# Mixing over 64 nodes as two 64-row products on the two halves of TensorE's rows

## The chip, the cores and the metric

The kernel runs on one core of one Trainium2 chip. The metric is the device time in microseconds of one execution, from the first to the last instruction. Before the change it was 2570.01 us (median of 3 runs, 2565.66 to 2570.18).

## The reference

The input `x` has 128 batches of 64 nodes with 256 features, and `adj` is one weighted 64 x 64 graph. Four graph layers follow one another, each of the form

```python
x = _layernorm(x + layer(x, adj))
```

What matters here is that each layer multiplies by a 64 x 64 matrix over the nodes, the same for every batch. Layer 0 does it three times, between three weight matrices (256 to 512 to 1024 to 256 features):

```python
def _slconv(x, adj, S, W):              # S is adj as well: weighting = adj * adj
    support = jnp.einsum('bnf,fh->bnh', x, W)
    weighting = adj * S
    return jnp.einsum('nm,bmh->bnh', weighting, support)
```

Layer 1 multiplies by the eigenvectors U of the graph's Laplacian (transposed, and back again), around two small dense layers. Layer 2 multiplies by `adj` twice, each time with a 256 x 256 weight and relu, and then runs LSTMs over windows of 1 to 4 nodes. Layer 3 is attention along the graph: scores h h^T within a batch, a softmax and a weighted sum. All arithmetic is in float32.

## The kernel before

**Tiles and groups.** The 8192 rows (128 batches x 64 nodes) are 64 tiles of 128 rows, so a tile holds two batches: batch h = 0 on the upper 64 partitions, h = 1 on the lower 64. Four tiles are a group, and there are 16 groups. `X` keeps all rows in on-chip memory for the whole kernel.

**Mixing.** Multiplying by the 64 x 64 matrix is called mixing. It is done for both batches of a tile at once, by a 128 x 128 matrix that has the 64 x 64 matrix twice on its diagonal and zeros elsewhere: `sqT2` (adj squared elementwise, transposed), `adT2`, `u2` and `ut2`. The transposed mixing, with which this case deals, takes 128 columns of features of a tile as the stationary operand (the weights that TensorE loads) and moves the 128 columns of the mixing matrix through. The result has features on the partitions and (tile, batch, node) along the free dimension, which is what the dense layer behind it needs. `mm` (L718) issues one product and adds its estimated time to `now[0]`, the planner's clock. A float32 product is two records in the profile, each with a weight load (`PEld`) and a matmul (`PE`).

**Where it occurs.** In layer 0, `mixed` (L750) makes one chunk of 128 features at a time: four products, one for each tile, fill a PSUM bank (`ps`, six of them), and ScalarE copies it out (L755). It runs with two chunks on X (into `m1`) and with four on `h1` (into `m2`). In layers 1 and 2, another `mixed` (L941) makes two chunks, eight products in two banks; VectorE copies one bank out (L951) and ScalarE the other (L952). It runs once with `u2` and twice with `adT2` in each group. So a group has 48 mixing products, and the 16 groups have 768.

**Another mixing, which stays.** At the end of layer 0 the mixing isn't transposed: `sqT2` is the stationary operand, and 512 columns are moved (`ps<-s,sqT` in the profile, issued right behind L855). Its results are added to X on VectorE (L861), and a layer norm on ScalarE follows.

**What sets the order.** TensorE's order is written out by a planner in Python (`manual_schedule`, L869 and L1195). Each group is a generator that issues some instructions and then yields the time on the planner's clock from which it may go on. In layer 0 two groups are under way at once, later three (`WAYS`). The planner always takes the first group that is due, and moves the clock on if none is. Delays such as `now[0] + 1.5` or `+ MIXED` leave time for copies, in which other groups fill TensorE. In layer 0, `between` (L708), which `mm` calls, threads in the instructions of an eigenvalue computation (`eigen`) that layer 1 needs. Its products are small, most of them on 128 rows and some on 64. In layer 0 VectorE's order is fixed by hand as well.

**A product of another shape.** The scores of layer 3 (L1140) are on 128 rows, but have 64 columns of weights, and write the upper or lower 64 partitions of a bank. They use the left and the right half of TensorE's columns.

Of the kernel before, what the change touches and what calls it, by code (L numbers as in the profile page):

```python
# [15 lines left out]
N = 64  # L16
# [516 lines left out]
P = 128  # L533
# [33 lines left out]
def scalar_norm(tc, pool, x, half, spare):  # L567


    nc = tc.nc  # L570
    S, G = nc.scalar, nc.gpsimd
    nm, va, rs, nb = (pool.tile([P, 2], F32, name=f"sn_{n}") for n in ("nm", "va", "rs", "nb"))

    def total(out, t, func, **kw):
        S.activation(spare[0](), x[:, t, :], func, accum_out=out[:, t:t + 1], **kw)  # L575

    def root():
        G.tensor_scalar(rs, va, 1.0 / D, EPS, op0=ALU.mult, op1=ALU.add)
        G.tensor_tensor(rs, rs, half[:, :2], ALU.pow)
        G.tensor_tensor(nb, nm, rs, ALU.mult)  # L580

    def apply(t):
        S.activation(x[:, t, :], x[:, t, :], AF.Identity, bias=nb[:, t:t + 1], scale=rs[:, t:t + 1])

    return ([lambda t=t: total(nm, t, AF.Identity, scale=-1.0 / D) for t in range(2)] +
            [lambda t=t: total(va, t, AF.Square, bias=nm[:, t:t + 1]) for t in range(2)] + [root] +
            [lambda t=t: apply(t) for t in range(2)])
# [8 lines left out]
def kernel(  # L596
# [26 lines left out]
    V, S, PE = nc.vector, nc.scalar, nc.tensor  # L623
    NT = ROWS // P
# [4 lines left out]
    def tl(pool, shape, tag, **kw):  # L629
        uid[0] += 1  # L630
        return pool.tile(shape, F32, tag=tag, name=f"{tag}_{uid[0]}", **kw)
# [9 lines left out]
    psa = phase_a.enter_context(tc.tile_pool(name="psa", bufs=1, space=bass.MemoryType.PSUM))  # L641
# [12 lines left out]
    for h in range(2):  # L654
        hs = slice(h * N, (h + 1) * N)
# [24 lines left out]
    sqT2 = keep.tile([P, P], F32, name="sqT2")  # L680
# [23 lines left out]
    now = [0.0]  # L704
# [3 lines left out]
    def between():  # L708
        while eig and eig[0] <= now[0]:
            try:  # L710
                eig[0] = next(eig[1])
            except StopIteration:
                eig.clear()
        if norms and due[0] <= now[0]:
            norms.pop(0)()
            due[0] = now[0] + 1.6

    def mm(out, lhsT, rhs, start=True, stop=True):  # L718
        PE.matmul(out, lhsT, rhs, start=start, stop=stop)  # L719
        now[0] += 2 * max(0.00084 * rhs.free_size(), 0.112)  # L720
        between()

    def run(out, pairs):
        for i, (lhsT, rhs) in enumerate(pairs):
            mm(out, lhsT, rhs, i == 0, i == len(pairs) - 1)

    def relu(dst, src):
        S.activation(dst, src, AF.Relu)  # L728
# [14 lines left out]
    def behind(name, g):  # L743
        while done[name] < g:
            yield now[0] + 0.3

    def layer0(g):
        xs = X[:, 4 * g:4 * g + 4, :]

        def mixed(dst, src, nf, more, then=None):  # L750
            for c in range(nf):
                p = tl(psa, [P, 512], "ps", bufs=6)
                for t in range(4):
                    mm(p[:, t * P:(t + 1) * P], src[:, t, c * P:(c + 1) * P], sqT2)
                S.copy(dst[:, c, :], p)  # L755
                if then and c == nf - 1:
                    done[then] = g
                yield now[0] + (more if c == nf - 1 else 0.0)

        yield from behind("first", g - 1)  # L760
        m1 = tl(pa, [P, 2, 512], "m1")
        yield from mixed(m1, xs, 2, 1.4)
        yield from behind("mixed", g - 1)
        h1 = tl(pa, [P, 4, 512], "h1")
        for t in range(4):
            p = tl(psa, [P, 512], "ps", bufs=6)
            run(p, [(m1[:, k, t * P:(t + 1) * P], aw1[:, k, :]) for k in range(2)])
            relu(h1[:, t, :], p)
            if t == 3:
                done["first"] = g  # L770
            yield now[0] + (2.1 if t == 3 else 0.0)
        if g == 0:
            VL.tensor_sub(T3, B22, B12)
            VL.tensor_sub(T1, B12, B11)
            VL.tensor_sub(T2, B22, T1)
            VL.tensor_sub(T4, T2, B21)
        yield from behind("second", g - 1)
        m2 = tl(pa, [P, 4, 512], "m2")
        yield from mixed(m2, h1, 4, 1.4, "mixed")
        A11, A12, A21, A22 = (m2[:, k:k + 2, r:r + 256] for r in (0, 256) for k in (0, 2))  # L780
        ss = tl(pa, [P, 4, 2, 256], "ss")
        S1, S2, S3, S4 = (ss[:, i] for i in range(4))
        VL.tensor_add(S1, A21, A22)
        VL.tensor_sub(S2, S1, A11)
        VL.tensor_sub(S3, A11, A21)
        VL.tensor_sub(S4, A12, S2)
        yield from behind("third", g - 1)
        h2 = tl(pa, [P, 8, 512], "h2")

        def product(w, a, j):  # L790
            p = tl(psa, [P, 2, 256], "ps", bufs=6)
            for i in range(2):
                cols = slice((2 * j + i) * P, (2 * j + i + 1) * P)
                run(p[:, i, :], [(w[:, k, cols], a[:, k, :]) for k in range(2)])
            return p

        def quarter(j, r, c):
            return h2[:, 4 * c + 2 * j:4 * c + 2 * j + 2, r * 256:(r + 1) * 256]

        def join(j, r, c, x, y, op=ALU.add):  # L800
            VL.tensor_tensor(quarter(j, r, c), x, y, op)
            relu(quarter(j, r, c), quarter(j, r, c))


        late = None
        for j in range(2):
            p1 = tl(pa, [P, 2, 256], "p1", bufs=2)
            u2, u3 = (tl(pa, [P, 2, 256], n) for n in ("u2", "u3"))

            def one(p, p1=p1):  # L810
                S.copy(p1, p)

            def six(p, p1=p1, u2=u2):
                VL.tensor_add(u2, p1, p)

            def seven(p, u2=u2, u3=u3):
                VL.tensor_add(u3, u2, p)

            def five(p, j=j, u2=u2, u3=u3):
                join(j, 1, 1, u3, p)  # L820
                VL.tensor_add(u2, u2, p)

            def four(p, j=j, u3=u3):
                join(j, 1, 0, u3, p, ALU.subtract)

            def three(p, j=j, u2=u2):
                join(j, 0, 1, u2, p)

            def two(p, j=j, p1=p1):
                join(j, 0, 0, p1, p)  # L830

            for then, w, a in ((one, B11, A11), (two, B21, A12), (six, T2, S2), (seven, T3, S3), (four, T4, A22),
                               (five, T1, S1), (three, B22, S4)):
                p = product(w, a, j)
                if norms:
                    norms.pop(0)()
                if late:
                    late[0](late[1])
                late = then, p
                if j == 1 and then is three:  # L840
                    done["second"] = g
                yield now[0]
        late[0](late[1])
        s3 = tl(pa, [P, 4, D], "s3")
        for t in (2, 0):
            p = tl(psa, [P, 2, D], "ps", bufs=6)
            for i in range(2):
                for k in range(0, 8, 4):
                    for c in range(k, k + 4):
                        mm(p[:, i, :], h2[:, c, (t + i) * P:(t + i + 1) * P], aw3[:, c, :], c == 0, c == 7)  # L850
                    if t + i == 1 and k == 4:
                        done["third"] = g
                    yield now[0]
            S.copy(s3[:, t:t + 2, :], p)
        yield now[0] + 1.5  # L855
        for t in (2, 0):
            p = tl(psa, [P, 2, D], "ps", bufs=6)
            mm(p, sqT2, s3[:, t:t + 2, :])
            yield now[0] + 0.4
            x2 = xs[:, t:t + 2, :]  # L860
            VL.tensor_add(x2, p, x2)  # L861
            norms.extend(scalar_norm(tc, small, x2, half, spare))
# [72 lines left out]
    def ps4(shape=(P, 512)):  # L935
        return tl(psb, list(shape), "ps")

    def as3(t, a):
        return t.rearrange("p (a b) -> p a b", a=a)

    def mixed(src, rhs, ready):  # L941

        dst = as3(work(), 2)
        ps = [ps4() for _ in range(2)]
        for t in range(4):
            if t % 2 == 0:
                yield ready[t // 2]
            for c in range(2):
                mm(ps[c][:, t * P:(t + 1) * P], src[:, t, c * P:(c + 1) * P], rhs)
        with tc.high_priority(offset=1500):  # L950
            V.tensor_copy(dst[:, 0, :], ps[0])  # L951
        S.copy(dst[:, 1, :], ps[1])  # L952
        yield now[0] + MIXED
        return dst

# [296 lines left out]
```

## Time and profile before

| | |
|---|---|
| median of 3 runs | 2570.01 us |
| span of the profiled execution | 2566.4 us |
| layer 0, from the start to about | 875 us |
| layers 1 to 3, from there to the end | 1691 us |
| granted TensorE clock, mean | 0.994 |
| mixing from X in layer 0, `sqT,X` | 256 records |
| mixing from h in layer 0, `sqT,h` | 512 records |
| mixing in layers 1 and 2, `u,X`, `adT,X` and `adT,w` | 256 records each |
| one such matmul, median | 275 ns |
| one such weight load, median | 192 ns |
| ScalarE copy of a bank in layer 0, L755 | 575 ns, 96 of them |
| VectorE and ScalarE copy of a bank later, L951 and L952 | 689 and 586 ns, 48 each |

How to read it: a line of a group or a timeline has the time, the engine, the line of the kernel, the operation, the tiles by name (`ps<-sqT,h` writes a PSUM tile from `sqT2` and `h1`), and then, for TensorE, rows x columns of the weights and the shape that is moved. `128*64 128x64` is 128 rows and 64 columns of weights, with 64 columns moved. The duration of a matmul runs from its issue to its end, while the next has been started; so 275 ns is not what it costs. The distance between starts is. In a merged line of the timeline the second number is the time from the start of its first record to the end of its last.

### The profile page before, as it was taken

The numbers are of one execution on the slowest core, as the hardware profiler recorded it, in microseconds if no ns is written. First come the engines' busy times: TensorE is split into PE (matmuls) and PEld (weight loads), VectorE is DVE, ScalarE is ACT, GpSimd is POOL, SyncE is SP. The second block draws the span as 40 slices with busy tenths as digits, with TensorE's granted clock in tenths as the row PEclk, the third lists the DMA queues.
The fourth block names the chain that finished last, engine by engine and source line by source line (L and its number), as shares of the span: only waits on it lengthen the run. The fifth ranks groups of instructions, "written<-read, shape, count | busy, mean of one in ns | idle before, by whom it ended". The sixth has DMA issues, their size and how long they took to land.

```text
span 2566.4 us, 39034 instructions
## 1 busy us (share of the span) xinstructions
PE 2502.8 (98%) x15020; PEld 2193.7 (85%) x15020; DVE 1414.7 (55%) x5001; ACT 1120.2 (44%) x2727; POOL 133.3 (5%) x316
## 2 busy tenths in 40 slices
PE   8999999999999999999999999999999999999996
PEld 7788887888877889889989889899898898978995
DVE  6877777778884433444453544534435445353235
ACT  3343333433333344544444454444444545445444
POOL 0000000000000100000000000000000000000001
PEclk9999999999999999999999999999999999999998
DMA  6000000000000300000000000000000000000000
GB/s 218 1 1 1 1 1 1 1 1 1 1 1 1 115 1 1 9 9 1 9 6 4 9 1 9 9 1 9 4 6 9 1 9 9 1 9 1 1 1 25
DMA packets 24811, 32.15 MB, mean 13 GB/s; under 512 B 2352, under 2 KB 21552, under 8 KB 24624
## 3 DMA queue, kind: packets, MB, share of 16 engines
q1 hardware_dynamic: 24384, 29.60, 3.4%
q8 instruction: 118, 1.93, 0.3%
q14 instruction: 69, 0.57, 0.1%
q10 hardware_dynamic: 240, 0.05, 0.0%
HBM read 21.25 MB, written 8.39 MB: 12 GB/s over the span
## 4 chain that ended last, share of the span: by engine, by line
PE 81%; DVE 10%; ACT 5%; POOL 2%; issue 1%; DMA 0%; ACTq 0%; POOLq 0%; DVEq 0%
PE ps L719 78%; POOL ln_rs L553 1%; DVE br L51 1%; DVE Q L51 1%; DVE X L563 1%; PE ps L924 1%; ACT gates L1027 1%; DVE ln_st L550 1%; DVE h L51 1%; PE ps L1140 1%; DVE D L51 1%; ACT spare L575 1%; ACT L1027 1%; ACT L1153 1%; DVE X L1090 1%
## 5 line engine op out<-in xcount | busy, mean ns | idle before, releaser
L719 PE MATMUL ps<-w,wih 128*128 128x128 f32 (+2 forms) x4992 | 895.1, 319 | 1.7 <-DVE w L1046 1.7
L719 PEld LDWEIGHTS ps<-w,wih 128*128 128x128 f32 x4992 | 764.5, 191 | 50.9 <-issue 8.4
L1027 ACT ACTIVATE gates<-ps,cbi 128x128 f32<-128x128 f32 (+2 forms) x1248 | 501.7, 409 | 581.9 <-PE ps L719 577.1
L719 PE MATMUL ps<-hs,whh 128*128 128x128 f32 (+2 forms) x3072 | 542.1, 303 | 4.4 <-DVE hs L1037 4.3
L719 PEld LDWEIGHTS ps<-hs,whh 128*128 128x128 f32 x3072 | 453.8, 191 | 33.8 <-issue 11.0
L1032 DVE TENSOR_TENSOR gates<-gates 128x128 f32<-128x128 f32 (+2 forms) x256 | 89.5, 350 | 253.9 <-ACT gates L1027 253.8
L719 PE MATMUL ps<-aw,h 128*128 128x256 f32 x1024 | 227.4, 379 | 0.1
L719 PEld LDWEIGHTS ps<-aw,h 128*128 128x128 f32 x1024 | 192.9, 190 | 26.7 <-ACT h L728 1.2
L728 ACT ACTIVATE h<-h 128x512 f32<-128x512 f32 x128 | 80.8, 631 | 240.3 <-DVE h L51 240.3
L1035 ACT ACTIVATE gates<-c 128x128 f32<-128x128 f32 (+2 forms) x288 | 98.3, 341 | 109.8 <-DVE c L1034 104.0
L1031 DVE TENSOR_TENSOR c<-c,gates 128x128 f32<-128x128 f32 (+2 forms) x192 | 62.5, 325 | 107.7 <-ACT gates L1027 105.3
L719 PE MATMUL ps<-aw,m 128*128 128x512 f32 x256 | 120.9, 593 | 0.0
L719 PE MATMUL ps<-ss,aw 128*128 128x256 f32 x512 | 118.0, 380 | 0.0
L719 PE MATMUL ps<-ss,tw 128*128 128x256 f32 x512 | 118.0, 380 | 0.0
L719 PE MATMUL ps<-m,aw 128*128 128x256 f32 x512 | 117.1, 379 | 0.0
L1046 DVE TENSOR_TENSOR w<-gates 128x256 f32<-128x256 f32 (+2 forms) x160 | 59.4, 377 | 102.3 <-PE ps L719 62.9
L1037 DVE TENSOR_TENSOR hs<-gates 128x128 f32<-128x128 f32 (+2 forms) x192 | 62.8, 328 | 92.6 <-ACT gates L1035 52.8
L563 DVE TENSOR_SCALAR X<-X,ln_mv,ln_rs 128x256 f32<-128x256 f32 x184 | 68.1, 411 | 82.2 <-POOL ln_rs L553 82.2
L719 PEld LDWEIGHTS ps<-m,aw 128*128 128x128 f32 x512 | 96.5, 190 | 18.9 <-issue 5.3
L719 PEld LDWEIGHTS ps<-ss,tw 128*128 128x128 f32 x512 | 96.2, 190 | 13.7 <-issue 1.0
L719 PEld LDWEIGHTS ps<-ss,aw 128*128 128x128 f32 x512 | 96.3, 190 | 12.8
L552 POOL TENSOR_SCALAR ln_rs<-ln_mv 128x2 f32<-128x2 f32 x96 | 23.1, 241 | 1573.0 <-DVE ln_mv L551 1571.2
(294 smaller groups left out, 3142.4 us busy)
## 6 DMA issues: line engine op xcount, KB each, us to landing
out_dram<-X SPq DMA_DIRECT2D x32, 256.0 KB, 2.1
X<-in_x_dram SPq DMA_DIRECT2D x31, 256.0 KB, 6.0
wih<-in_c_ih_dram SPq DMA_DIRECT2D x4, 1024.0 KB, 7.2
aw<-in_a_w_dram SPq DMA_DIRECT2D x3, 1024.0 KB, 9.6
whh<-in_c_hh_dram SPq DMA_DIRECT2D x3, 1024.0 KB, 9.3
aw<-in_a_w_dram SPq DMA_DIRECT2D x1, 512.0 KB, 4.9
cw<-in_c_w_dram SPq DMA_DIRECT2D x2, 256.0 KB, 3.6
X<-in_x_dram SPq DMA_DIRECT2D x2, 128.0 KB, 2.2
```

What stands on the lines that cost most here:

```text
L51: return getattr(self.engine, name)(out, *args, **kw)
L550: nc.vector.bn_stats(st[:, t, :], x[:, t, :])
L553: nc.gpsimd.tensor_tensor(rs, rs, half[:, :n], ALU.pow)
L563: nc.vector.tensor_scalar(x[:, t, :], x[:, t, :], mv[:, t, 0:1], rs[:, t:t + 1], op0=ALU.subtract, op1=ALU.mult)
L719: PE.matmul(out, lhsT, rhs, start=start, stop=stop)
L728: S.activation(dst, src, AF.Relu)
L1027: S.activation(gate[q][:, h, :], pp, AF.Tanh if q == "g" else AF.Sigmoid, bias=bias[:, j:j + 1])
L1031: V.tensor_mul(c[:, h, :], c[:, h, :], gate["f"][:, h, :])
L1032: V.tensor_mul(to, gate["i"][:, h, :], gate["g"][:, h, :])
L1035: S.activation(gate["i"][:, h, :], c[:, h, :] if p > 1 else to, AF.Tanh)
L1037: V.tensor_mul(new[:, h, :], gate["o"][:, h, :], gate["i"][:, h, :])
L1046: V.tensor_mul(hT[:, h, slice(first + p - 1, first + nw * p, p), :], gate["o"][:, h, :].rearrange("p (w b) -> p w b", b=8), gate["i"][:, h ...
```

## The change

A mixing product becomes two, one for each batch of the tile. Each takes 64 of the 128 rows: the 64 partitions of one batch as weights (still 128 feature columns), and the 64 x 64 block of the mixing matrix as the moved operand. The two use the upper and the lower half of TensorE's rows, and write two different banks. The zeros off the diagonal are no longer multiplied. It is meant to let both halves work at once, with half as many columns moved.

What goes with it: `mix` adds 0.12 us to the planner's clock for the two products, and the eigenvalue instructions are threaded in behind all products of a pair of chunks only. In layer 0 the chunks are taken in pairs, since a bank now holds one batch of two chunks; the copies write runs of 64 elements. The delay in front of the last mixing of layer 0 goes from 1.5 to 6.5 us on the planner's clock (for all groups but the last), and the 0.4 between its two products is dropped. This moves it behind other work, so that more transposed mixings stand next to one another. In layers 1 and 2 each of the two copies now takes one batch instead of one chunk.

```diff
+    def mix(outs, rows, both):
+        for h in range(2):
+            hs = slice(h * N, (h + 1) * N)
+            PE.matmul(outs[h], rows[hs, :], both[hs, hs], start=True, stop=True)
+        now[0] += 0.12
...
         def mixed(dst, src, nf, more, then=None):
-            for c in range(nf):
-                p = tl(psa, [P, 512], "ps", bufs=6)
-                for t in range(4):
-                    mm(p[:, t * P:(t + 1) * P], src[:, t, c * P:(c + 1) * P], sqT2)
-                S.copy(dst[:, c, :], p)
-                if then and c == nf - 1:
+            to = dst.rearrange("p c (t h n) -> p h c t n", h=2, n=N)
+            for c in range(0, nf, 2):
+                ps = [tl(psa, [P, 2, 4, N], "ps", bufs=6) for _ in range(2)]
+                for i in range(2):
+                    for t in range(4):
+                        mix([p[:, i, t, :] for p in ps], src[:, t, (c + i) * P:(c + i + 1) * P], sqT2)
+                between()
+                for h in range(2):
+                    S.copy(to[:, h, c:c + 2], ps[h])
+                if then and c == nf - 2:
...
-        yield now[0] + 1.5
+        yield now[0] + (1.5 if g == NT // 4 - 1 else 6.5)
         for t in (2, 0):
             p = tl(psa, [P, 2, D], "ps", bufs=6)
             mm(p, sqT2, s3[:, t:t + 2, :])
-            yield now[0] + 0.4
+            yield now[0]
...
     def mixed(src, rhs, ready):
         dst = as3(work(), 2)
-        ps = [ps4() for _ in range(2)]
+        to = dst.rearrange("p c (t h n) -> p h c t n", h=2, n=N)
+        ps = [ps4((P, 2, 4, N)) for _ in range(2)]
         for t in range(4):
             if t % 2 == 0:
                 yield ready[t // 2]
             for c in range(2):
-                mm(ps[c][:, t * P:(t + 1) * P], src[:, t, c * P:(c + 1) * P], rhs)
+                mix([p[:, c, t, :] for p in ps], src[:, t, c * P:(c + 1) * P], rhs)
         with tc.high_priority(offset=1500):
-            V.tensor_copy(dst[:, 0, :], ps[0])
-        S.copy(dst[:, 1, :], ps[1])
+            V.tensor_copy(to[:, 0], ps[0])
+        S.copy(to[:, 1], ps[1])
```

More of the change, by code (lines that the diff above doesn't have):

```diff
@@ L750, in mixed @@
         def mixed(dst, src, nf, more, then=None):
-            for c in range(nf):
-                p = tl(psa, [P, 512], "ps", bufs=6)
-                for t in range(4):
-                    mm(p[:, t * P:(t + 1) * P], src[:, t, c * P:(c + 1) * P], sqT2)
-                S.copy(dst[:, c, :], p)
-                if then and c == nf - 1:
+            to = dst.rearrange("p c (t h n) -> p h c t n", h=2, n=N)
[8 more added lines that the diff above has]
+                if then and c == nf - 2:
                     done[then] = g
-                yield now[0] + (more if c == nf - 1 else 0.0)
+                yield now[0] + (more if c == nf - 2 else 0.0)
         yield from behind("first", g - 1)
```

## The prediction

> **What bounds the kernel now.** I read the busy table first, then the chain of work that ended last, then one stretch of the windows view, to see whether TensorE's busy share is real work or an average over stages.
>
> ```profile
> PE 2502.8 (98%) x15020; PEld 2193.7 (85%) x15020; DVE 1414.7 (55%) x5001; ACT 1120.2 (44%) x2727; POOL 133.3 (5%) x316
> ...
> PE 81%; DVE 10%; ACT 5%; POOL 2%; issue 1%; DMA 0%; ACTq 0%; POOLq 0%; DVEq 0%
> ```
> ```profile
> 500.00:750.00 250.00, 247.19 (x1168) 201.39 (x1167) 208.78 (x758) 88.38 (x206) 10.88 (x30) 1.00 0.00 1
> ...
> 1500.00:2000.00 500.00, 494.14 (x3296) 448.71 (x3295) 231.97 (x653) 237.99 (x572) 28.45 (x60) 1.00 0.02 6
> ```
>
> TensorE (first busy number) is at 99% in the first layer (500 to 750) and in the later ones (1500 to 2000), at full clock. So a microsecond more or less in its queue is a microsecond of the kernel, and the question is how long one product holds the queue. A duration doesn't tell (products are pipelined); the distance between starts does, so I went to the timeline. First the old mixing product:
>
> ```profile
> 399.75 1.50 PE L719 MATMUL ps<-sqT,h 128*128 128x128 f32 x12
> 401.09 1.88 PE L719 MATMUL ps<-aw,m 128*128 128x512 f32 x4
> ```
>
> Twelve records take from 399.75 to 401.09: 111.7 ns each. An f32 product leaves two records, so a mixing product costs 0.223 us. It loads 128 columns of weights and moves 128 columns. Which of the two sets the 112 ns? Two other shapes answer. The scores of layer 3 (L1140) load 64 columns on all 128 rows, and go by turns to the left and right half of the columns:
>
> ```profile
> 1034.84 0.49 PE L924 MATMUL ps<-ident,w 128*128 128x128 f32 x3
> 1035.26 1.20 PE L1140 MATMUL ps<-w 128*64 128x64 f32 x32
> 1036.39 1.13 PE L719 MATMUL ps<-w,wih 128*128 128x256 f32 x4
> 1037.36 1.03 PE L719 MATMUL ps<-hs,whh 128*128 128x256 f32 x4
> ```
> ```profile
> 2523.57 0.73 PE L1140 MATMUL ps<-w 128*64 128x64 f32 x16
> ```
>
> 32 records last 1.20 us, 16 last 0.73: 8 pairs more cost 0.47, 58.5 ns a pair. The halves of the columns therefore do run side by side, each at 58.5 ns a record. The second shape is a small product of the eigenvalue code, on 64 rows:
>
> ```profile
> L93 PE MATMUL pc<-de,eig_c x4: 193/204/214, 521.6 to 524.6; 64*64 64x1 f32 x4
> ```
> ```profile
> 521.57 0.19 PEld L93 LDWEIGHTS pc<-de,eig_c 64*64 64x64 f32 x2 [0.33 <-issue]
> ```
>
> It moves one column, yet its second load starts 0.19 - 0.13 = 0.055 us after the first (0.13 is what one load lasts in the view of this tile). So with nothing to move, and on 64 rows only, 64 columns of weights still need about 54 ns. Halving the rows did not halve the load. Both fit one rule, 0.83 ns a column plus 5: 58 ns for 64 columns, 112 for 128. The old mixing is at the limit of its loads.
>
> **What the Trainium skill says.** "TensorE: Matmul & The Clock Gate", LDWEIGHTS, has the time of a load go with its columns and not with its rows, P / 1.2 ns: 53 ns for 64 and 107 for 128. The 55 ns on 64 rows agree. "TensorEngine Tiling (Array Packing)", Key Properties, says that tiles work independently, loads included, and that a change of tiling mode drains the engine. Independence is seen above for halves of the columns; no run here shows it for halves of the rows. The drain is seen: the three transposes start 0.109 apart and the last starts at 1035.06, so the scores could have started at 1035.17, but do at 1035.26. Behind them L719 starts at 1036.39 instead of 1036.30. The same page (Gotcha 1) has row tiles write to different banks, which the change does.
>
> **The change part by part.**
>
> *The products.* Removed: 768 mixing products (16 groups x 48: 8 and 16 in layer 0, three times 8 later), 1536 records x 111.7 ns = 171.6 us of TensorE's queue. Added: 1536 products on 64 rows, 3072 records, as two streams of 1536. Each record still loads 128 columns of weights, for `rows[hs, :]` is the weight and has all 128; only the moved side shrinks to 64. The unknown is the time of one slot (a record in each half). Bounds: 58.5 ns, the row of L1140, if the load were no limit; 2 x 111.7 if the halves took turns at loading. I take 111.7: the loads of the two halves at once, each as long as before. Then the sum is 171.6 again, and the part is worth **0**.
>
> *Changes of mode.* In the order in which the built program's instructions stand on TensorE, the 64-row products form 65 unbroken runs (20 in layer 0, most of them 8 and 16 mixings in one; 45 later). The price of a run is read off the scores, which are one themselves: from where they could have started (1035.17) to where the next full product counts as started. That is 1036.39 + 0.10, because its 4 records last 1.13 and the next 4 last 1.03: its first load is bare. 1.32 us, less 16 slots x 0.0585 = 0.94, is 0.384; I use 0.39, to which a run of 16 records comes as well. In a 64-row run the first bare load is twice as wide, 0.05 more: 0.44. 65 x 0.44 = **+28.6 us**, all of it on TensorE. If waits for data fall together with the drains it is less; I keep 0.39 (25.4) and 0.50 (32.5) as ends.
>
> *Evacuation.* Layer 0 still makes 96 ScalarE copies of 512 elements (575 ns each), now two behind each pair of chunks, in runs of 64. The last chunk is ready one copy later, 0.6 us. Queued behind it is the next consumer of m1 or m2. In the new order another group's mixing, four 512-wide records (1.7 us) or, for m2, a first product that needs only chunks 0 and 1 stand in between. ScalarE is 35% busy in that stretch (88 of 250). Cost 0. In layers 1 and 2 VectorE and ScalarE still take one copy each after the last product: 0.
>
> *The wait of 6.5 and the two yields without 0.4.* They reorder: the two 512-wide products with sqT2 now follow eight 512-wide products of the other group instead of standing between them, which lets mixings join. TensorE waits for nothing there before (its idle time ahead of these products is 0.0), so nothing is won but fewer runs, which are counted already.
>
> *Planner and pools.* `mix` counts 0.12 us where I expect 0.22, so the plan runs ahead of the chip: operands are ready earlier than TensorE needs them, not later. The eigenvalue code ends 40 products ahead of the end of layer 0 in the new order (144 before), still inside. Two banks of six are held per mixing, and the copies free them within 1.2 us: 0.
>
> Sum: 2570.0 + 0 + 28.6 = 2598.6, rounded to **2599**.
>
> **The rivals.**
>
> *Slots at the rate of the moved side (faster).* If loading on 64 rows took half the time, or hid behind the other half, a slot would be 58.5 ns as in L1140: 1536 x 58.5 = 89.9, 81.7 saved. The drains stay, 65 x 0.39 = 25.4. 2570.0 - 81.7 + 25.4 = **2514**. For it: the planner's 0.12 is two slots of that kind, and column halves reach it. Against: their loads are 64 columns wide, and the 55 ns on 64 rows.
>
> *Load and move no longer overlap within a half.* A slot is 107 + 54 = 161 ns, 247 in all: 2570.0 + 75.7 + 28.6 = **2674**. The first product after each change does behave so, but only the first.
>
> *The halves take turns at loading.* 3072 x 111.7 = 343.1: 2570.0 + 171.6 + 28.6 = **2770**. Against: column halves load side by side, 32 loads in 1.06 us. For: those are different columns, while the row halves fill the same ones.
>
> *Waits swallow the drains.* All gaps between TensorE's starts beyond its pace sum to about 73 us before, by my sum over the trace, 10 of them in layer 0's mixing, which waits for relu'd h. If most drains fell into such gaps, it would end at **2572**.
>
> **How the numbers follow.** Load-bound with drains 56%; moved-side rate 28%; no overlap 7%; turns 5%; swallowed drains 4%. The predicted time is that of the first. The range goes from 2508 (below the fast rival, with a few us of reordering) to 2612 (drains at 0.50, slots at 115 ns), which leaves out the two dear rivals, 12%, and the tails. Faster by over 0.2% is the fast rival and a sliver: 0.29; within 0.2% the swallowed drains: 0.04; slower the rest: 0.67.
>
> **What would show it.** In the profile after, a 64-row run's records must come two in 112 ns; 8 mixings must last about 1.8 us plus the tail. Weight loads of this form should last near 182 to 190 ns. The first full product after a run should stand some 0.09 us late and be 0.10 longer. TensorE's busy share stays at 97% or more. A slot near 58 ns would overthrow the first step, the claim that a load doesn't shrink with its rows; one near 224 the second, that the halves load at once. If slots come at 112 and the time is still not up, the price of a run is wrong.

## The result, and the profile after

The changed kernel takes 2582.59 us (median of 4, 2582.1 to 2583.5) against a median of 2569.8 for the kernel before in the same comparison. By the means of all runs that is 1.0054 of it, 95% interval 1.0036 to 1.0071. It is 13 us slower, where 29 were forecast. The direction held, the size did not. From run to run the kernel before takes 2564 to 2572 us, at a granted clock of 0.996 at the short end and 0.993 at the long one, so a few us between two medians can be clock alone.

First the page of the changed kernel, with the busy shares and the chain of work that ended last:

```profile
PE 2522.0 (98%) x16556; PEld 2197.6 (85%) x16556; DVE 1410.9 (55%) x5001; ACT 1125.9 (44%) x2727; POOL 134.8 (5%) x316
...
PE 90%; DVE 4%; ACT 3%; POOL 2%; issue 1%; DMA 0%; ACTq 0%; POOLq 0%; DVEq 0%
PE ps L719 80%; PE ps L728 7%; PE ps L937 2%; POOL ln_rs L553 1%; DVE X L563 1%; DVE ln_st L550 1%; PE ps L1154 1%; PE pc L93 1%; ACT gates L1041 1%; DVE X L1104 1%; ACT L1167 1%; ACT att L1167 0%; POOL ln_rs L552 0%; DVE ln_mv L551 0%; ACT gates L1049 0%
```

TensorE has 1536 more records and is still the bound; the 64-row products (L728) have 7% of the chain. The windows view of the same two stretches (busy time of TensorE first) shows layer 0 fuller than before, 250.00 of 250 against 247.19, and the later layers emptier, 490.85 of 500 against 494.14:

```profile
500.00:750.00 250.00, 250.00 (x1419) 203.04 (x1418) 199.15 (x740) 93.70 (x218) 11.66 (x30) 1.00 0.00 1
1500.00:2000.00 500.00, 490.85 (x3477) 441.94 (x3477) 228.71 (x649) 233.98 (x563) 28.19 (x60) 1.00 0.02 6
```

So there are two stories, and the view of single tiles dates the border between them. `u,X` is the first mixing of layer 1: its first start is the end of layer 0. The line before and the line after:

```profile
L719 PE MATMUL ps<-u,X x256: 273/275/377, 876.1 to 2267.8; 128*128 128x128 f32 x128
```
```profile
L728 PE MATMUL ps<-u,X x512: 271/272/321, 870.9 to 2286.2; 64*128 64x64 f32 x171
```

Layer 0 ends 5.2 us earlier than before (876.1 to 870.9), though it has 20 of the 65 changes of mode. The other layers take 2580.3 - 870.9 = 1709.4 instead of 2566.4 - 876.1 = 1690.3, 19.1 more. Now the timeline of a run of 64-row products in layer 2, and one in layer 0:

```profile
2325.18 1.03 PE L719 MATMUL ps<-w,wih 128*128 128x256 f32 x4
2326.13 1.11 PE L728 MATMUL ps<-adT,w 64*128 64x64 f32 x16
2327.17 1.13 PE L719 MATMUL ps<-w,wih 128*128 128x256 f32 x4
```
```profile
452.92 2.00 PE L728 MATMUL ps<-sqT,X 64*128 64x64 f32 x32
454.75 3.74 PE L728 MATMUL ps<-sqT,h 64*128 64x64 f32 x64
458.42 1.98 PE L719 MATMUL ps<-aw,m 128*128 128x512 f32 x4
```

The second run has 96 records, from 452.92 to 454.75 + 3.74 = 458.49: 5.57 us. The first has 16 and lasts 1.11. 40 slots more cost 4.46: 111.5 ns a slot, and 111.7 by the mean distance of the starts in all runs of the trace. A slot holds a record in each half, and the old product needed 111.7 for one record of full size. So the halves run side by side, and nothing is gained.

The price of a run: without it the next full product would have followed at 2325.18 + 4 x 0.216 = 2326.04. The product behind it counts as started at 2327.17 + 0.10 (its 4 records last 1.13, four of the same shape 1.03). 1.23 less 8 slots of 0.112 is 0.34. The run of 96 comes to the same, and nearly every other in the trace too; those that don't have a wait in them.

### The profile page after: what moved, and what is told of

Same layout as the page of the kernel before. It is cut to its first block, busy times and chain, and to the rows that moved or that the text cites. A ratio compares the mean times of both kernels' runs of the same rounds, so it can differ in the third digit from the quotient of the medians.

```text
span 2580.3 us, 42132 instructions
## 1 busy us (share of the span) xinstructions
PE 2522.0 (98%) x16556; PEld 2197.6 (85%) x16556; DVE 1410.9 (55%) x5001; ACT 1125.9 (44%) x2727; POOL 134.8 (5%) x316
## 4 chain that ended last, share of the span: by engine, by line
PE 90%; DVE 4%; ACT 3%; POOL 2%; issue 1%; DMA 0%; ACTq 0%; POOLq 0%; DVEq 0%
PE ps L719 80%; PE ps L728 7%; PE ps L937 2%; POOL ln_rs L553 1%; DVE X L563 1%; DVE ln_st L550 1%; PE ps L1154 1%; PE pc L93 1%; ACT gates L1041 1%; DVE X L1104 1%; ACT L1167 1%; ACT att L1167 0%; POOL ln_rs L552 0%; DVE ln_mv L551 0%; ACT gates L1049 0%
## 5 line engine op out<-in xcount | busy, mean ns | idle before, releaser
L719 PE MATMUL ps<-w,wih 128*128 128x256 f32 (+2 forms) x4992 | 895.6, 319 | 1.7 <-DVE w L1060 1.7
L719 PEld LDWEIGHTS ps<-hs,whh 128*128 128x128 f32 x3072 | 454.4, 191 | 34.7 <-DVE hs L1051 11.4
L563 DVE TENSOR_SCALAR X<-X,ln_mv,ln_rs 128x256 f32<-128x256 f32 x184 | 68.2, 410 | 83.1 <-POOL ln_rs L553 83.1
```

Of the source, the lines that this page charges most:

```text
L563: nc.vector.tensor_scalar(x[:, t, :], x[:, t, :], mv[:, t, 0:1], rs[:, t:t + 1], op0=ALU.subtract, op1=ALU.mult)
```

## The experiments

Each was compared with the kernel before on the same chip; that one's median lay between 2569.3 and 2569.7. The ratios are of means, so they can differ a little from those of the medians. The last three columns are from one profile each: the first start of `u,X`, the rest of the span, and what half clock took from layer 0 and from the rest. For the last I add up the time for which the trace has TensorE at half of its clock, and take half of it; this is an estimate.

| kernel | median us | ratio to before, 95% interval | layer 0 ends | rest | half clock took |
|---|---|---|---|---|---|
| before | 2569.8 | | 876.1 | 1690.3 | 1.7 + 13.1 |
| changed | 2582.6 | 1.0054 [1.0036, 1.0071] | 870.9 | 1709.4 | 0 + 13.3 |
| e1 reordering alone | 2552.9 | 0.9949 [0.9936, 0.9962] | 864.5 | 1686.3 | 0 + 9.9 |
| e2 64-row products alone | 2594.0 | 1.0107 [1.0091, 1.0122] | 882.6 | 1709.4 | 8.5 + 15.2 |
| e13 delay of 6.5 alone | 2556.2 | 0.9948 [0.9934, 0.9962] | 863.2 | 1691.5 | 0 + 14.8 |
| e14 without the 0.4 alone | 2561.8 | 0.9974 [0.9965, 0.9983] | 867.9 | 1691.2 | 0 + 14.8 |
| e3 clock 0.224 | 2573.2 | 1.0020 [1.0011, 1.0029] | 871.2 | 1697.8 | 0 + 12.2 |
| e6 clock 0.30 | 2660.7 | 1.0360 [1.0346, 1.0374] | 879.8 | 1783.8 | 3.4 + 37.2 |
| e5 clock 0.12 on e1 | 2556.6 | 0.9956 [0.9943, 0.9968] | 861.9 | 1694.4 | 0 + 11.5 |
| e4 four quarters | 2544.0 | 0.9909 [0.9895, 0.9922] | 859.0 | 1683.0 | 0 + 18.7 |
| e7 quarters, longer delays | 2542.8 | 0.9898 [0.9884, 0.9911] | 859.2 | 1679.3 | 1.7 + 16.8 |
| e8 quarters, still longer | 2541.2 | 0.9891 [0.9877, 0.9904] | 857.9 | 1680.3 | 0 + 16.5 |
| e9 quarters in layers 1 to 3 | 2549.5 | 0.9926 [0.9914, 0.9938] | 864.9 | 1683.3 | 0 + 18.7 |
| e10 as e9, clock 0.16 | 2566.4 | 0.9991 [0.9982, 0.9999] | 865.0 | 1702.6 | 0 + 28.8 |
| e11 quarters in layer 0 | 2550.2 | 0.9931 [0.9919, 0.9944] | 857.8 | 1690.2 | 0 + 13.1 |
| e12 as e8, copies shared | 2558.4 | 0.9961 [0.9947, 0.9975] | 875.0 | 1682.4 | 8.5 + 18.3 |

e1, e13 and e14 have the code of before in layers 1 to 3, and TensorE's order there is the same in all four traces. Yet their rests lie between 1686.3 and 1691.5. That spread is clock: less what half clock took, the four are 1677.2 (before), 1676.4, 1676.7 and 1676.4. So the last column has to be taken off before two profiles are compared.

Half clock also makes a wait dearer than it is long. TensorE's clock is granted at half for stretches of 3.4 to 10.2 us. There are 69 of them in the sixteen traces, not counting the last 75 us of each, and every one begins within 5 us of the start of a gap of 0.7 us or more between two of TensorE's products. Most gaps of that size have no such stretch behind them, and what decides it is not shown. In e2 it happens twice in layer 0; here is the second time:

```profile
830.65 5.47 PE L728 MATMUL ps<-sqT,h 64*128 64x64 f32 x52 [1.36 <-ACT h L736]
831.00:841.00 10.00, 10.00 (x62) 8.48 (x61) 3.65 (x8) 4.76 (x11) 1.07 (x3) 0.50 0.01 2
```

TensorE waited 1.36 us for relu'd h. The 52 records behind the wait are 26 slots and would last about 3.1 us at 111.7 ns a slot; at half clock (the 0.50 in the second line, the windows view) they last 5.47.

### Where 16 us of the forecast went: e1 and e2

e1 is the kernel before with the reordering:

```diff
-        yield now[0] + 1.5
+        yield now[0] + (1.5 if g == NT // 4 - 1 else 6.5)
...
-            yield now[0] + 0.4
+            yield now[0]
```

> The kernel before with the reordering alone: the delay ahead of the last mixing of layer 0 goes from 1.5 to 6.5 and the 0.4 between its two products is dropped; the mixing products are the old full ones. Theory A (the 9 us that the changed kernel is better than its 65 runs at 0.34 us each come from this reordering, which takes away TensorE's waits for relu'd h in layer 0): 2570 - 9 = 2561. Rival B (the drains of the mode changes fall into waits that were there anyway, and the reordering gives nothing): 2570. Rival C (the give-back is the mixing itself, whose chunks come in pairs, or the planner's clock): 2570.

e2 is the changed kernel with this taken back.

> The changed kernel without the reordering: 1.5 and 0.4 as before. Its 64-row products form 67 runs instead of 65, so the mode changes cost 22.8 us by the trace's 0.34. Theory A: 2582.6 + 9 + 0.7 = 2592. Rivals B and C: 2583.

Rivals B and C fall in both, and theory A has the direction, though not the size in e1: that kernel is 13 us faster than before by the ratio (10 to 16 by the interval, 16 by the medians), where 9 were expected. e2 is 11.4 slower than the changed kernel. The reordering brings the border of the layers forward by 876.1 - 864.5 = 11.6 with the old products, and by 882.6 - 870.9 = 11.7 with the new.

That these two agree is chance, for they are made of different things. With the old products 1.7 us are half clock and 9.9 are waits. With the new ones 8.5 are half clock, 2.0 are waits for relu'd h, and two runs fewer give 0.7. The clock isn't the accident of one profile: it was 0.990 to 0.992 in all four runs of e2, and 0.994 or 0.995 in all of the changed kernel's. Nor is e2's 882.6 - 876.1 = 6.5 simply the price of its 22 runs in layer 0, some 7.5. It has 6.8 more of half clock as well, and some 7.8 less of waits: the 64-row products alone already wait less for relu'd h.

What TensorE waits for is in the view of waits, from 500 to 875 us (total us, times, longest; the weight loads of PEld and the products of PE wait in part at the same time). The kernel before:

```profile
PEld ps L719 <- ACT h L728: 9.3, 9, 2.9
PE ps L719 <- ACT h L728: 6.9, 5, 2.8
```

e1, where the second line is gone, and e2 (to 880 us):

```profile
PEld ps L719 <- ACT h L728: 1.3, 4, 0.4
```
```profile
PE ps L728 <- ACT h L736: 2.0, 2, 1.4
```

So the h mixing waited for ScalarE's relu of h, L728 of the kernel before.

### Which edit of the reordering: e13 and e14

> The kernel before with the delay of 6.5 alone; the 0.4 stays. Theory D (the delay does it: the two last mixings stand between the 512-wide products and the mixing of h, which so waits less for relu'd h): as e1, 2553 to 2557. Rival (the dropped 0.4): 2569.

> The kernel before with the 0.4 dropped alone; the delay stays at 1.5. Theory D: 2567 to 2570. Rival: 2553 to 2557.

The delay does it: e13 is as good as e1 within the intervals. It doesn't do it by distance, though, as its theory had it. From the end of the last 512-wide product to the h mixing there are 1.75 us on average in e13, and 1.76 before. What differs is ScalarE's queue. Before, and then e13:

```profile
664.32 1.09 ACT L583 ACTIVATE X<-X,sn_nb,sn_rs 128x256 f32<-128x256 f32 x2 [0.82 <-POOL sn_nb L580]
665.32 0.57 ACT L728 ACTIVATE h<-ps 128x512 f32<-128x512 f32 x1
665.94 1.27 PE L719 MATMUL ps<-sqT,h 128*128 128x128 f32 x9 [1.25 <-ACT h L728]
```
```profile
657.80 0.60 ACT L728 ACTIVATE h<-ps 128x512 f32<-128x512 f32 x1 [1.12 <-PE ps L719]
659.38 0.42 ACT L575 ACTIVATE spare<-X 128x256 f32<-128x256 f32 x1 [0.99 <-DVE X L51]
```

Before, the relu of the last operand stood behind steps of the layer norm (L575, L583) that the last mixings set off, and the norm itself waited 0.82 us for GpSimd; TensorE stood for 1.25. In e13 the relu comes first and the norm after it. Over the 16 groups this relu starts 1.45 us after its product on average before, at worst 3.24; in e13 0.34, with no norm step ahead of it in any group.

But dropping the 0.4 alone takes 7.6 us too, for which the theory gave nothing. In e14 TensorE's wait for relu'd h is still there, at 2.7 us instead of 6.9, and the norm still stands ahead of the relu, but holds it up for 1.75 us at most. The two edits don't add up, since both move the same wait.

### The planner's clock: e3, e6 and e5

```diff
-        now[0] += 0.12
+        now[0] += 0.224
```

> The changed kernel with the planner's clock told the measured time of a mixing, 0.224 instead of 0.12. 62 runs instead of 65, 1 us less by the price of 0.34. Theory A (the clock's lag moves nothing that TensorE waits for): 2581 to 2583. Rival C in its form that the lagging clock gives the 9 us back: 2590.

e3 is 9.4 us faster than the changed kernel, and 8 below the least that theory A allowed. Layer 0 doesn't move (871.2); the gain is in the rest, 1709.4 to 1697.8. Of these 11.6 us half clock is 1.1 and six runs fewer there are 2.0, so some 8.5 are waits. Next 0.30:

> The changed kernel with 0.30 on the planner's clock for a mixing. Its 64-row products form 100 runs instead of 65 (62 with 0.224), since other groups are let in between the two halves of a mixing. The price of a run by the trace is 0.34 us: against e3's 2573.2, 38 x 0.34 = 12.9 more, 2586. With the price of the prediction, 0.44: 2590. If the drains fell into waits: 2573 to 2577.

It missed by 75 us. The price of a run is not the reason: two thirds of the 100 runs come to 0.34 in the trace as well, but others have waits of up to 2.5 us in them or behind. Against e3 the rest is 86 us longer, of which half clock is 25. The waits of TensorE in e6:

```profile
PE ps L719 <- ACT w L736: 17.3, 6, 3.1
PE ps L719 <- DVE hs L1051: 12.1, 13, 1.5
PE ps L719 <- ACT w L966: 11.8, 6, 2.0
PE ps L719 <- DVE w L965: 11.5, 7, 2.3
```

My reading is that with 0.30 the planner's clock is ahead of the chip, so that the order puts consumers where their operands (L965 and L966 are the copies of a mixing) are not made yet. A clock that lags should then be harmless. e5 tries that without the 64-row products: e1 with 0.12 for each old mixing product.

> The kernel of e1 (old full mixing products, new delays), with the planner's clock advanced by 0.12 instead of 0.224 for each transposed mixing product, and nothing else. e3 against the changed kernel showed 9.4 us for this clock with the 64-row products in place. Theory L (a clock that runs behind TensorE moves consumers nearer to their producers and makes waits by itself): 2553 + 5 to 12 = 2558 to 2565. Rival P (e3's gain is the luck of one order of the three groups, or belongs to the 64-row products alone): 2553, within 3.

By the medians it is 3.7 us slower than e1, between the two theories. The profiles say more: layer 0 ends 2.6 earlier, and the rest is 8.1 longer, of which half clock is 1.6. So the lag does cost some 6.5 us of waits in the later layers, with the old products too, against the 8.5 that e3 wins. That speaks for theory L there, but each clock is one order of three groups, and I can't tell a rule from these runs: 0.12, 0.224 and 0.30 give three orders, and each has its own waits.

### Is it the load? Four quarters: e4

If 128 columns of weights set the slot, cutting the columns too must shorten it. Each 64-row product is cut into two of 64 weight columns, on the quarters of the array:

```diff
-            PE.matmul(outs[h], rows[hs, :], both[hs, hs], start=True, stop=True)
+            for q in range(2):
+                qs = slice(q * N, (q + 1) * N)
+                PE.matmul(outs[h][qs], rows[hs, qs], both[hs, hs], start=True, stop=True)
```

> The changed kernel with each 64-row product cut again into two of 64 weight columns, so that a mixing is four products on the four quarters of the array; everything is still computed. If a slot is bound by the columns of its weight load, and four quarters work at once as two halves do: a slot is 58.5 ns instead of 111.7, 1536 x 53.2 = 81.7 us less, 2582.6 - 81.7 = 2501. Rival: the queue feeds no more than the densest seen so far, two records in 58 ns; then the 8 records of a mixing take 234 ns instead of 223, 2582.6 + 8 = 2591. Rival: the load isn't the bound, but some fixed time of a record on 64 rows, 111.7 ns: 2583 with four quarters at once, 2754 with two at a time.

The rivals fall at once. The timeline of e4:

```profile
1002.65 0.69 PE L730 MATMUL ps<-adT,w 64*64 64x64 f32 x32
1138.81 0.65 PE L730 MATMUL ps<-u,X 64*64 64x64 f32 x32
1154.58 1.16 PE L730 MATMUL ps<-adT,w 64*64 64x64 f32 x64
```

The first and the last line are whole runs; the middle one continues a run. 32 records last 0.69 and 64 last 1.16, so 8 slots more take 0.47: 58.4 ns for a slot of four records, by the mean distance of the starts in the trace. The load of 64 columns takes half the time of 128, and the four quarters work at once; a record every 15 ns can be fed. TensorE's work falls by the 82 us expected, but the kernel only by 38.6, because the gaps between its products grow.

### Where the quarters lose: e7, e8, e9, e10, e11 and e12

e7 and e8 lengthen the planner's delays behind a mixing (layer 0 from 1.4 to 2.4 and 3.4, later from 1.2 to 1.6 and 2.2).

> e4 (four quarters) with the planner's delays behind a mixing raised: in layer 0 from 1.4 to 2.4, later from 1.2 to 1.6. 72 runs. e4's trace has TensorE's work 82 us below the changed kernel's, but 43 us more gaps, most of them behind a mixing, where the next product waits for the two copies. Theory W (the copies come one after the other on one engine, and the delays are too short for them): half of the gaps go, 2544 - 20 + 2 = 2526. Rival (ScalarE is the bound of that stretch: six copies of 0.58 us against 2.8 us of mixing): 2540 to 2546, whatever the delays.

> As e7, with delays of 3.4 in layer 0 and 2.2 later. 71 runs. Theory W: 2515 to 2526. Rival: 2540 to 2546.

The rival is right: they bring 1 and 3 us. I then took ScalarE's copies in layer 0 for the cause, and split the quarters by layers.

> The kernel of e1 (old full mixing and new delays in layer 0) with the four quarters of e4 in layers 1 to 3 alone: 384 mixings, 45 runs of small products. By slot and price: 2552.9 - 384 x (0.2234 - 0.1168) + 45 x 0.34 = 2552.9 - 40.9 + 15.3 = 2527. Theory S (e4's missing 40 us are lost in layer 0, where ScalarE has to copy 3.5 us of banks during 2.8 us of mixing): 2525 to 2532. Rival (they are lost wherever quarters stand): 2545 or more.

> As e9, with 0.16 instead of 0.12 on the planner's clock, which is 0.117 for the slots and 0.34 / 8 for the change of mode: the clock then keeps step with TensorE. 39 runs. If the clock's step matters as from the changed kernel to e3: below e9 by the 2 us of the runs and another 3 to 8. If e9's clock is close enough: 2 us below e9.

> The complement: four quarters in layer 0 alone, old full products later. 384 mixings, 20 runs. By slot and price 2552.9 - 40.9 + 6.8 = 2519. Theory S: the waits for ScalarE's copies take nearly all of it, 2545 to 2555. Rival (loss wherever quarters stand): 2535.

Theory S is half right. e11, with quarters in layer 0 alone, ends it at 857.8; the slots and 20 runs should have brought e1's 864.5 down by 34, so 27 are lost. None of it is half clock. e4's trace does show waits for the copies there, in the first line of its waits in layer 0; for the second the profile names nothing that it waits for:

```profile
PE ps L719 <- ACT m L769: 12.0, 17, 1.8
PE ps L730 <- issue: 7.2, 7, 1.4
```

But e9, with quarters in layers 1 to 3 alone, loses too: its rest is 1683.3 where 1690.3 - 25.6 = 1664.7 was due, 18.6 more, of which half clock is 5.6. Its longest waits are for the LSTM's state, a layer norm (L563) and the attention, not for the copies:

```profile
PE ps L719 <- DVE hs L1048: 11.5, 11, 1.9
PE ps L934 <- DVE X L563: 9.5, 5, 5.3
PE ps L934 <- ACT att L1164: 8.8, 9, 2.4
```

I read this as TensorE's work coming near the chains of the other engines: with less of it to fill in, each chain's latency shows. No run tests that alone. e10 then gave the planner's clock its honest value, and became 17 us slower instead of faster. With this order TensorE waits 27 us for the norms, where e9 waits 9.5, and of the 19.3 us by which its rest is longer half clock is 10.1:

```profile
PE ps L934 <- DVE X L563: 27.2, 19, 5.3
PE ps L719 <- DVE w L962: 10.3, 11, 3.4
```

A planner's clock in step with the chip is thus no recipe. At last e12, which moves a third of layer 0's copies to VectorE:

> e8 (four quarters, longer delays) with 32 of the 96 copies of layer 0's mixing moved from ScalarE to VectorE: the second one behind X, and the second one behind the last pair of chunks of h. Theory S in its narrower form (in layer 0 TensorE waits behind the mixing for ScalarE, which has two copies of 0.58 us in a row): some 0.6 us less behind each of 32 runs, 2541 - 10 to 19 = 2522 to 2531. Rival (VectorE, which is at three quarters in layer 0 and has the eigenvalue chain in its fixed order, is no better): 2541 or above.

The rival holds: layer 0 ends at 875.0 instead of 857.9, half of it (8.5) by half clock. VectorE, with the eigenvalue chain in its fixed order, is the worse place for them. e8, at 2541.2 us, 0.9891 [0.9877, 0.9904] of before, is the fastest version found, though not told apart from e7, and beats both kernels.

## Why the prediction was off

**The slot was right.** "A record in each half", bounded by a load of 128 columns, 111.7 ns: measured 111.7. That a load doesn't shrink with its rows, read off one small product of the eigenvalue code, and that halves load side by side, read off the scores, both hold. e4 shows the bound from the other end, 58.4 ns with 64 columns. The three rivals that touched the slot (58.5, 161 and 224 ns) are out.

**The price of a run was sized too high**: 0.44 forecast, 0.34 measured, in 65 runs 28.6 against 22.1. The failing step is "In a 64-row run the first bare load is twice as wide, 0.05 more", on top of a 0.39 that held for the scores alone. The starts in the trace show that the second slot of a 64-row run comes 160 ns behind the first, 48 more than a slot; in the scores it is 107, 49 more. The wider load costs no more. And in the scores' run one half of the columns falls a slot behind the other on the way, some 0.05 that belongs to the scores and not to a change of mode. The rest agrees: 0.09 ahead of the run, about 0.10 behind it, and 0.10 in the bare load of the next full product.

**The reordering was priced at 0 and is worth 11.6 us to the kernel before.** This is the larger term, and the second step that failed. It said that "TensorE waits for nothing there before", since the idle time ahead of the two last mixings is 0.0. That is the wrong product to look at. What the delay moves is the layer norm that the last mixings set off: on ScalarE it stood ahead of the relu that the h mixing waits for, and the waits of the kernel before had 6.9 us of that. The prediction even counted it, "10 of them in layer 0's mixing", but only as a place where drains might vanish. In part they did: the 64-row products without the reordering (e2) wait 2.0 us for relu'd h. So the rival of the swallowed drains was not all wrong in layer 0.

**Planner and pools were priced at 0.** The copies of the changed kernel were hidden nearly as the step said (one wait of 1.1 us in layer 0). In the later layers 45 x 0.34 = 15.3 was due and 19.1 measured; of the 3.8 us left half clock is 0.2, and the others are an order of the three groups with other waits. e3 removes them, and more. "Operands are ready earlier than TensorE needs them" does not fit e3 and e5, where a planner's clock of 0.12 instead of 0.224 costs some 8.5 and 6.5 us of waits; e10 shows that the honest clock is not always the better one.

Together: the 65 runs are 22.1. In layer 0 they are 6.8, and yet it ends 5.2 earlier, so 12.0 came back there: 1.7 of half clock and 10.3 of waits, of which the view of waits has 8.9. In the later layers 3.8 came on top. 22.1 - 12.0 + 3.8 = 13.9, the difference of the two profiles (13 by the medians). The 12.0 and the 3.8 are what is left when the runs are taken off; e1's 11.6 is the independent check of the first, and the second has none.

**What stays open.** Why 0.224 instead of 0.12 takes some 8.5 us of waits from layers 1 to 3 under the 64-row products, and 0.16 instead of 0.12 adds 9.2 us besides half clock under the quarters. Each is one order of three interleaved groups; the waits that differ are listed by the trace, but no run isolates a cause. Open too is why half clock follows some of TensorE's waits and not others.

## What to carry to other kernels

Before an array is split, ask which operand sets the pace of a product: here the columns of the weight load did, and halving rows and moved columns touched neither; only cutting the weight columns as well gave the factor of two. Price a change of mode from a run of the same program, but from its ends, slot by slot, and count unbroken runs and not products. When one change carries a second, price each at the wait it moves, and look for that wait on every engine's queue: here the small reordering won back nearly half of the 25 us that the main idea cost by itself (e2 against before). And before two profiles are compared, take off what the granted clock took: here it made up most of one difference that looked like the effect of an edit.

## What the runs showed of the hardware

Two row halves, each loading 128 columns, take 111.7 ns a slot, the same as one full record. Four quarters of 64 x 64 take float32 records at one every 15 ns, each with its own weight load; the array does four of them in the 58.4 ns of a slot, where the scores need 58.5 for two records of 64 columns. A run in another tiling costs 0.34 us for 64 x 128 (16 to 96 records) and about 0.35 for 64 x 64 (32 to 192 records), whatever its length, where no wait falls into it: 0.09 ahead of it and about 0.10 behind it, 0.05 in its second slot and 0.10 in the first load of the next full product.

TensorE's clock was granted at half for 3.4 to 10.2 us at a time; each such stretch ahead of the last 75 us began within 5 us of the start of a gap of 0.7 us or more in TensorE's products.
